# A two-layer graph network on one core: index work and layer 1's folds moved behind layer 0's table, the table's rows moved into x's memory, three x loads issued by ScalarE, and superchunks 3 to 5 gathered in place

## The chip, the cores and the metric

The kernel runs on one core of a Trainium2 chip. The metric is device time in microseconds (us) of one execution; three runs of the kernel before took 4008.17, 4010.82 and 4012.63 us. Changes are judged against the median, 4010.82.

TensorE (PE) multiplies, VectorE (DVE) and ScalarE (ACT) do element-wise work, GpSimd (POOL) here mainly issues gathers by index, and SyncE (SP) issues plain transfers. Each engine works through its own instructions in order and waits for others by semaphores.

## What is computed

There are 6250 nodes with 256 features, and 200000 edges sorted by destination, each with 32 attributes. The reference, cut to what matters:

```python
h = jnp.maximum(_layernorm(x, axis=-1), 0.0)

def _gat(x, src, dst, ea, Wg, a_s, a_d, Wge, a_e, b, n, h, f):
    hx = (x @ Wg).reshape(n, h, f)
    he = (ea @ Wge).reshape(-1, h, f)
    al = jax.nn.leaky_relu(jnp.einsum('nhf,hf->nh', hx, a_s)[src] + jnp.einsum('nhf,hf->nh', hx, a_d)[dst] + jnp.einsum('ehf,hf->eh', he, a_e), 0.2)
    m = jax.ops.segment_max(al, dst, num_segments=n)
    al = jnp.exp(al - m[dst])
    al = al / jax.ops.segment_sum(al, dst, num_segments=n)[dst]
    out = jax.ops.segment_sum(hx[src] * al[:, :, None], dst, num_segments=n)
    return out.reshape(n, h * f) + b

# per layer: te = relu(edge_attr @ We + be) * exp(x @ Wo + bo)[src], self loops added,
# layer 0 (4 heads): x = relu(_gat(...) + x); layer 1 (1 head): x = _gat(...) + x
x = x + (layer 1's x + h)
```

So each layer needs, for every edge, the row of its source node (`hx[src]` and a few numbers beside it), a softmax over the edges of one destination, and a weighted sum.

## The kernel before

**Prologue (`prologue`, L219).** The nodes are 49 tiles of 128 (`NT`), taken in groups of up to seven (`GT`), nine groups in all: tiles 0-1, 2-6, 7-13, 14-20, 21-27, 28-34, 35-41, 42-46 and 47-48. Per tile: layer norm statistics on VectorE (`stats`: bn_stats L292, bn_aggr L295, then an inverse square root by three Newton steps, on VectorE or for some groups on GpSimd, L307 to L325), normalisation and relu on ScalarE (`norm`, L337), two transposes on TensorE (`turn`, L343) and their copy on ScalarE (L345), a product with the weights (`mult`, L471), and the addition of the bias into a row block `trow` on VectorE (`keep`, L475). When a group is complete, `store` takes two exponentials on ScalarE (L360, L361) and writes the block into layer 0's table T0 in HBM (L362, on SP). The x blocks are loaded by SP (`load`, L241): six at the start and three more when a buffer comes free.

The edges are 1563 chunks of 128, in 66 superchunks of up to 24 chunks (C). Superchunk 0's source rows are not fetched from the table: GpSimd gathers their x from the input (`first_rows`, L275) into the buffer `G0`, and tiles 49 to 72 (groups 9 and 10) compute their rows in the same way, into `G0` itself.

`fold` (L187) and `fold_e` (L202) multiply attention vectors into the weights: four or two transposes, a ScalarE copy, a few small products, small copies on VectorE. `indices` (L477) and `index_group` (L630) load index tables and make the masks, offsets and flags that the edge loop needs, on VectorE; two of their results, `locrow` and `flags`, go to HBM and come back by `load_lb` and `load_fl`. These pieces are generators: the loop over tiles calls `next` on them at set values of its counter k, and so writes out by hand what stands between the tiles on each engine. In iteration k, tile k+3 is normalised, k+1 turned, k multiplied and k-1 kept.

**Edge loop (`edges`, L679).** A step is one superchunk of one layer. `gather` (L962) issues one indirect transfer per chunk on GpSimd, 128 rows of the table into the step's buffer G. There are three buffers (`gath0` to `gath2`), used in turn; `gath1` and `gath2` lie on memory that the prologue's pools had. Normally a step's first gather waits until the buffer's former step is done with all of it, that is with its sums; a step with `own` instead writes into that very tile, and each chunk's gather waits only for what used that chunk. Before, step 3 of layer 0 is such a step. VectorE makes one-hot matrices (`onehots`, L1163) and scaled rows (`scale`, L1334), and TensorE sums a step's edges into its nodes by one product a chunk (`sums`, L1353). Step k+1 is gathered while step k is computed. `ending` (L793) handles the last three superchunks a, b, c of a layer together and starts the next layer; layer 1's table T1 is written there by `rows3`.

Of the kernel before, what the change touches and what calls it, by code (L numbers as in the profile page):

```python
# [22 lines left out]
F32 = mybir.dt.float32  # L23
# [56 lines left out]
class Kernel:  # L80
# [138 lines left out]
    def prologue(self):  # L219
# [7 lines left out]
        with ExitStack() as c:  # L227
            xp = self.pool("x", 1, c)
            wp = self.pool("pw", 2, c)
# [6 lines left out]
            def load(g):  # L236
                if g < g0:
# [3 lines left out]
                    nc.sync.dma_start(x, a["x"][0:NT * P, :].rearrange("(p t) d -> p t d", p=P)[:, ts[0]:ts[0] + n, :])  # L241
# [26 lines left out]
            trows = [wp.tile([P, GT, L.TW], F32, name=f"trow{i}", bufs=1) for i in range(3)]  # L268
# [15 lines left out]
            def stats(g):  # L284

                n, x = len(groups[g]), xs[g]
                w = GT if g < g0 else C
                st = wp.tile([P, w, 6], F32, name=f"st{w}", bufs=2 if g < g0 else 1)
                mv = wp.tile([P, w, 2], F32, name=f"mv{w}", bufs=3 if g < g0 else 1)
                s = wp.tile([P, 3, w], F32, name=f"sc{w}", bufs=3 if g < g0 else 1)  # L290
                for i in range(n):
                    V.bn_stats(st[:, i, :], x[:, i, :])  # L292
                    yield
# [12 lines left out]
                e = nc.gpsimd if 3 <= g <= g0 else V  # L306
                for _ in range(3):  # L307
                    e.tensor_mul(t, y, y)
                    if e is V:
                        yield  # L310
                    e.tensor_mul(t, t, v)
                    if e is V:
                        yield
                    if e is V:
                        V.scalar_tensor_tensor(y, t, 1.5, y, op0=OP.add, op1=OP.mult)
                        yield
# [49 lines left out]
            ahead = {g: stats(g) for g in range(1, len(groups))}  # L366
# [4 lines left out]
            def step(g):  # L371

                for q in list(ahead):
                    if q > g if q < g0 else k < (16 if q == g0 else NT):
                        continue
# [7 lines left out]
            for k in range(-3, len(tiles) + 1):  # L383
                if k == 6:
# [7 lines left out]
                if k == 8:  # L392
# [8 lines left out]
                if k in (14, 26, 32):  # L401
                    drain(folds.pop())
                if k == 26:
# [1315 lines left out]
```

## Time and profile before

| | us |
|---|---|
| runs | 4008.17, 4010.82, 4012.63 |
| profiled execution | 4009.49 |
| its span | 4007.7 |
| GpSimd busy in the span | 3000.5 |
| TensorE busy | 2654.4 |
| VectorE busy | 2446.4 |
| ScalarE busy | 1120.2 |

A row of the groups gives line, engine, operation, output and inputs, count, then busy time and mean of one in ns, then the idle time just before them on that engine and what ended it. A row of the timeline gives start and duration in us, engine and line, and in brackets the idle time before with what ended it. A product in float32 runs as two passes and counts twice (x4 for two products). Times are counted from the span's start.

### The profile page before, as it was taken

To read this page: it belongs to the slowest core of one execution; us is meant where nothing else is said; L and a number is where in the kernel's file an instruction comes from. 1 tells how busy PE (TensorE), PEld (TensorE's weight loads), DVE (VectorE), ACT (ScalarE), POOL (GpSimd) and SP (SyncE) were. 2 spreads that over 40 slices of the span, in tenths; PEclk is the share of its full clock that TensorE was granted. 3 is DMA by queue.
4 is the path that set the end of the run, shared out by engine and by line. 5 is a ranking of instruction groups with operands and counts; after the bars stand their busy time and mean duration, and the time that the engine had idled before them with its cause. 6 is when DMAs were issued, how large, how long until landed. Compare 5 with 4: busy or idle time off the path is not lost. (4 is left out here: it accounts for less than half of the span.)

```text
span 4007.7 us, 37932 instructions
## 1 busy us (share of the span) xinstructions
PE 2654.4 (66%) x10018; PEld 1741.3 (43%) x10018; DVE 2446.4 (61%) x6074; ACT 1120.2 (28%) x2676; POOL 3000.5 (75%) x3264
## 2 busy tenths in 40 slices
PE   8777676676666666666786666666565665665665
PEld 6444444444444444444454343343343343343343
DVE  7798877877877877877874443443443443443445
ACT  6211111111111111111124343343343343343341
POOL 6777777777777777777777777777777777777775
PEclk9888888888888888888898777777777777777777
DMA  7555555555555555555555445445445545545553
GB/s 245 139 163 150 154 160 147 152 160 148 151 161 149 151 160 150 151 160 149 153 168 144 132 138 143 134 138 145 132 139 143 134 138 144 132 138 143 133 139 97
DMA packets 248103, 592.01 MB, mean 148 GB/s; under 512 B 65851, under 2 KB 105329, under 8 KB 247643
## 3 DMA queue, kind: packets, MB, share of 16 engines
q0 software_dynamic: 150144, 422.75, 40.8%
q1 hardware_dynamic: 97197, 166.49, 13.0%
q8 instruction: 86, 1.41, 0.1%
q14 instruction: 132, 1.08, 0.1%
q10 hardware_dynamic: 544, 0.28, 0.0%
HBM read 544.19 MB, written 45.46 MB: 147 GB/s over the span
## 5 line engine op out<-in xcount | busy, mean ns | idle before, releaser
L971 POOL DMA_INDIRECT G<-T,src x3078 | 2923.8, 950 | 949.6 <-issue 898.1
L1353 PE MATMUL u<-G,S 128*128 128x270 f32 (+1 forms) x6226 | 1567.4, 415 | 192.1 <-DVE G L1324 190.7
L1353 PEld LDWEIGHTS u<-G,S 128*128 128x128 f32 x6226 | 1275.5, 206 | 483.3 <-DVE G L1324 217.4
L1343 ACT ACTIVATE G<-G,kw 128x256 f32<-128x256 f32 x1512 | 609.0, 496 | 0.0
L1072 ACT ACTIVATE R<-y,webd 128x1024 f32<-128x1024 f32 (+2 forms) x264 | 235.5, 892 | 1274.9 <-PE y L1071 795.2
L1250 PE MATMUL lf<-ident,fb 128*36 128x128 f32 (+1 forms) x132 | 49.8, 377 | 766.2 <-DVE fb L1243 764.0
L1226 DVE TENSOR_TENSOR G<-rt,G 128x96 f32<-128x96 f32 (+1 forms) x132 | 30.3, 229 | 806.7 <-DMA G<-T,src 806.1
L1334 DVE TENSOR_TENSOR G<-G,kps 128x6144 f32<-128x6144 f32 (+3 forms) x79 | 441.0, 5593 | 0.0
L1163 DVE TENSOR_TENSOR S<-kps,loc 128x3072 f32<-128x3072 f32 x132 | 437.6, 3315 | 4.6
L1071 PE MATMUL y<-ea,webd 64*128 64x256 f32 (+1 forms) x1056 | 386.0, 825 | 50.2 <-ACT R L1072 50.2
L1080 PE MATMUL zad<-R,wea 128*64 128x384 f32 (+1 forms) x1056 | 301.7, 712 | 157.8 <-ACT R L1072 157.6
L1250 PEld LDWEIGHTS lf<-ident,fb 128*36 128x36 f32 (+1 forms) x132 | 15.7, 119 | 807.2 <-DVE fb L1243 804.1
L1080 PEld LDWEIGHTS zad<-R,wea 128*64 128x64 f32 x1056 | 86.5, 185 | 418.0 <-ACT R L1072 333.7
L1358 ACT ACTIVATE U<-u 128x270 f32<-128x270 f32 (+1 forms) x131 | 51.5, 393 | 631.6 <-PE u L1353 631.6
L1385 DVE SCALAR_TENSOR_TENSOR mg<-U,mw 128x1 f32<-128x1 f32 x66 | 14.6, 221 | 281.1 <-ACT mw L1383 281.1
L1071 PEld LDWEIGHTS y<-ea,webd 64*128 64x128 f32 x1056 | 123.0, 285 | 122.1 <-ACT R L1072 68.8
L1316 DVE SCALAR_TENSOR_TENSOR G<-U,kw,G 1x257 f32<-1x257 f32 x62 | 29.6, 477 | 184.3 <-ACT G L1343 184.3
L1212 DVE STREAM_TRANSPOSE rt<-zad 128x768 f32<-128x768 f32 (+1 forms) x130 | 126.0, 970 | 5.0 <-PE zad L1198 5.0
L471 PE MATMUL fin<-wg,h1T 128*128 128x260 f32 x264 | 122.6, 611 | 3.6 <-ACT h1T L1445 3.6
L1184 PE MATMUL zad<-a,Q 128*128 128x12 bf16 (+1 forms) x132 | 25.9, 197 | 148.5 <-DVE a L1179 148.1
L1095 DVE TENSOR_TENSOR lb<-lb,kps 128x1536 bf16<-128x1536 bf16 (+1 forms) x68 | 112.9, 1661 | 0.0
L1455 ACT ACTIVATE t1row<-t1row 128x1 f32<-128x1 f32 x66 | 13.4, 203 | 354.1 <-DVE t1row L475 354.0
(231 smaller groups left out, 2349.1 us busy)
## 6 DMA issues: line engine op xcount, KB each, us to landing
G<-T,src POOLq DMA_INDIRECT x3078, 2.8
ea<-in_ea_dram SPq DMA_DIRECT2D x64, 768.0 KB
lb<-locrow SPq DMA_DIRECT2D x64, 384.0 KB
nd<-t1row SPq DMA_DIRECT2D x66, 225.8 KB
tw<-nd SPq DMA_DIRECT2D x66, 225.8 KB
tw<-T SPq DMA_DIRECT2D x66, 117.2 KB
T<-t1row SPq DMA_DIRECT2D x66, 113.8 KB
tw<-in_x_dram SPq DMA_DIRECT2D x66, 112.0 KB
```

The source lines that it names most:

```text
L471: self.nc.tensor.matmul(ps[:, :L.MW], hT[:, k, :], self.wg[L.l][:, k, :], start=(k == 0), stop=(k == 1))
L971: nc.gpsimd.indirect_dma_start(out=G[:, c, 0:L.TW], out_offset=None, in_=st.get("from", self.T[L.l])[0:self.N, :], in_offset=bass.Indirect ...
L1071: nc.tensor.matmul(y[:, i, :n], self.webd[l][r, :], ea[r, w], start=True, stop=True)
L1072: nc.scalar.activation(R[:, :, w], y[:, :, :n], AF.Relu, bias=self.be[l])
L1080: nc.tensor.matmul(st["zad"][i * PH:(i + 1) * PH, o], self.wea[l][0], R[:, i, w], start=True, stop=False)
L1095: V.tensor_tensor(lb[:, :, :n], lb[:, :, :n], self.k_part.unsqueeze(2).to_broadcast([P, i, n]), op=OP.is_equal)
L1163: nc.vector.tensor_tensor(st["S"][:, c0:c1, :], self.k_iota.unsqueeze(1).to_broadcast(w), self.loc[:, o + c0:o + c1].unsqueeze(2).to_broad ...
L1212: V.transpose(rv[:, :32 * c].rearrange("p (b n) -> p b n", b=2), z.rearrange("p (b n) -> p b n", b=2)[:, :, :16 * c])
L1250: self.nc.tensor.transpose(self.lf[0:e.shape[1], 1:P + 1], e, self.ident)
L1334: nc.vector.tensor_tensor(v, v, pw[:, c0:c1, :].unsqueeze(3) .to_broadcast([P, c1 - c0, H, L.F]), op=OP.mult)
L1343: self.nc.scalar.activation(v, v, AF.Copy, scale=st["w"][:, c:c + 1])
L1353: nc.tensor.matmul(st["u"][:, :L.W], S[:, i, :], G[:, i, 0:L.W], start=(j == 0), stop=(j == c - 1))
```

## The change

- `trows`, the three row blocks, are allocated in x's pool instead of the working pool.
- `load` issues the blocks 6 to 8 on ScalarE's queue, right behind the normalisation that frees their buffer.
- `stats` takes several groups at once: groups 7, 8 and 9 (13 tiles) become one; the inverse root of group 3 runs on VectorE, of groups 4 to 9 on GpSimd, of group 10 (18 tiles of superchunk 0) on VectorE as before, and that group's statistics begin at k = 45.
- The index loads move from k = 6 to k = 28, the index steps on VectorE to after k = 50; the three folds beside the table (k = 12, 24, 30) move to k = 53, 56 and 61; three idle products of 512 columns are put at k = 1.
- The last row block of the table is kept and stored first thing in iteration 49.
- The gathers of x rows for superchunk 0 come earlier in GpSimd's order.
- Steps 3, 4 and 5 of layer 0 gather in place into the buffers of steps 0, 1 and 2.
- In `ending`, the second half of the next layer's `rphase1` (`drain(y)`: two products and a relu of 1024 columns) moves from ahead of superchunk b's rows to behind superchunk c's.

```diff
             xp = self.pool("x", 1, c)
+            trows = [xp.tile([P, GT, L.TW], F32, name=f"trow{i}") for i in range(3)]
...
-                    nc.sync.dma_start(x, a["x"][0:NT * P, :].rearrange("(p t) d -> p t d", p=P)[:, ts[0]:ts[0] + n, :])
+                    q = nc.scalar if g > 5 else nc.sync
+                    q.dma_start(x, a["x"][0:NT * P, :].rearrange("(p t) d -> p t d", p=P)[:, ts[0]:ts[0] + n, :])
...
-            def stats(g):
+            def stats(*gs):
...
-                e = nc.gpsimd if 3 <= g <= g0 else V
+                e = nc.gpsimd if 4 <= g <= g0 else V
...
-            ahead = {g: stats(g) for g in range(1, len(groups))}
+            q = max(g0 - 2, 2)
+            ahead = {g: stats(g) for g in range(1, q)}
+            ahead[q] = stats(*range(q, g0 + 1))
+            for g in range(g0 + 1, len(groups)):
+                ahead[g] = stats(g)
...
-                if k == 6:
+                if k == 28:
                     next(index)
...
-                if k > 16 and k % 2 or k > NT:
+                if k > NT + 1:
                     next(index, None)
-                if k == 5:
+                if k == 1:
+                    idle(3)
+                if k == 34:
                     more()
...
-                if k in (12, 24, 30):
-                    folds.append(fold(self.L[1], pt) if k == 24 else fold_e(self.L[k // 30], pt))
+                f = k - NT
+                if f in (4, 7, 12):
+                    folds.append(fold(self.L[1], pt) if f == 7 else fold_e(self.L[f // 12], pt))
                     next(folds[0])
...
+                if f == 0:
+                    keep(*tiles[k - 1])
+                    while kept < g0:
+                        store(kept)
+                        kept += 1
+                    self.load_ea(0)
...
-                    if i == 0:
-                        if g > 2:
-                            load(g + 3)
...
+                    if g > 1 and i == len(groups[g]) - 1:
+                        load(g + 4)
...
-                if 0 <= k < 10 or k >= 14 and k % 4 == 0:
+                if k < 9 or k >= 14 and k % 2:
                     next(rows0, None)
-                if k == max(NT - 6, 7):
+                if f == 12:
                     while not hasattr(self, "flags"):
                         next(index)
                     next(index)
+                    self.load_lb(0)
+                    self.load_fl(0)
...
-        if len(steps) > 3 and steps[3]["L"].l == 0:
-            steps[3]["own"] = self.G0
...
+            if 3 <= k + 1 < 6 and nx["L"].l == 0:
+                nx["own"] = steps[k - 2]["G"]
             self.gather(nx)
...
         if after:
             self.rows3(a)
-        drain(y)
         self.rows1(b)
...
         self.rows3(c)
+        drain(y)
```

TensorE around tile 13 before, the place of layer 0's `fold_e` (`wge` is its weight, `h` and `hT` a normalised tile and its transpose, `ps` a product's bank):

```order
L471 MATMUL ps<-wg_99,hT 128x266 x2
L182 MATMUL pT<-ident,wge 128x128 x2
L209 MATMUL ps<-att_100,hT 128x4 x2
L343 MATMUL pT<-ident,h 128x128 x2
L471 MATMUL ps<-wg_99,hT 128x266 x2
```

And now at tiles 52 to 57, behind the table's 49 tiles:

```order
L479 MATMUL ps<-wg_102,hT 128x266 x2
L182 MATMUL pT<-ident,wge 128x128 x2
L209 MATMUL ps<-att_103,hT 128x4 x2
L340 MATMUL pT<-ident,h 128x128 x2
L479 MATMUL ps<-wg_102,hT 128x266 x2
L340 MATMUL pT<-ident,h 128x128 x2
L479 MATMUL ps<-wg_102,hT 128x266 x2
L340 MATMUL pT<-ident,h 128x128 x2
L479 MATMUL ps<-wg_102,hT 128x266 x2
L182 MATMUL pT<-ident,wg_882 128x128 x4
L194 MATMUL ps<-att_883,hT 128x2 x4
```

Between tiles 2 and 48 nothing but the tiles' own transposes and products stands on TensorE now.

VectorE at the end of the table, before (`trow` receives a table tile, `G` a tile of superchunk 0; slink, qd and low are index results):

```order
L561 TENSOR_TENSOR slink<-sc_389 1x66
L475 TENSOR_TENSOR trow_198<-ps,bias_105 128x266
L475 TENSOR_TENSOR trow_199<-ps,bias_105 128x266
L567 TENSOR_TENSOR qd_1223<-scf 1x264
L569 TENSOR_TENSOR low<-sc_389 1x66
L475 TENSOR_TENSOR trow_199<-ps,bias_105 128x266
L292 BN_STATS st_1235<-G 128x6 x4
```

And now:

```order
L483 TENSOR_TENSOR trow_82<-ps,bias_108 128x266
L294 BN_STATS st_1056<-G 128x6 x4
L483 TENSOR_TENSOR trow_82<-ps,bias_108 128x266
L294 BN_STATS st_1056<-G 128x6 x4
L483 TENSOR_TENSOR G<-ps,bias_108 128x266
L294 BN_STATS st_1056<-G 128x6 x2
L297 BN_AGGR mv_1057<-st_1056 128x2 x8
L504 CAST scf<-sc_782 128x726
```

The statistics of superchunk 0's later tiles stand ahead of the last table tile's addition, and the first index step (L504) behind it.

GpSimd's first gathers of layer 0, one row per step from step 1 on, with buffer numbers; before:

```order
L971 DMA G_1655<-T0_60,src_165 128x268 x24
L971 DMA G_1776<-T0_60,src_165 128x268 x24
L971 DMA G_201<-T0_60,src_165 128x268 x24
L971 DMA G_2085<-T0_60,src_165 128x268 x24
L971 DMA G_2254<-T0_60,src_165 128x268 x24
L971 DMA G_2429<-T0_60,src_165 128x268 x24
```

And now:

```order
L979 DMA G_1612<-T0_60,src_168 128x268 x24
L979 DMA G_1733<-T0_60,src_168 128x268 x24
L979 DMA G_201<-T0_60,src_168 128x268 x24
L979 DMA G_1612<-T0_60,src_168 128x268 x24
L979 DMA G_1733<-T0_60,src_168 128x268 x24
L979 DMA G_2384<-T0_60,src_168 128x268 x24
```

Steps 4 and 5 now write into the same tiles as steps 1 and 2 (G_1612, G_1733) instead of new ones; step 3 into superchunk 0's (G_201) as before; from step 6 on each step has a new tile again.

More of the change, by code (lines that the diff above doesn't have):

```diff
@@ L267, in prologue @@
                 nc.sync.dma_start(self.T[0][NT * P:N + P, :], zero[:N + P - NT * P, :L.TW])
-            trows = [wp.tile([P, GT, L.TW], F32, name=f"trow{i}", bufs=1) for i in range(3)]
             ln = wp.tile([P, NT + CX, 2], F32, name="ln", bufs=1)
@@ L282, in prologue @@
                 next(rows0, None)
-            def stats(g):
[L286 to L293, printed above, removed]
+            def stats(*gs):
+                n, g = sum(len(groups[g]) for g in gs), gs[0]
+                w = GT if n <= GT else C
+                st = wp.tile([P, w, 6], F32, name=f"st{w}", bufs=2)
+                mv = wp.tile([P, w, 2], F32, name=f"mv{w}", bufs=3 if w < C else 2)
+                s = wp.tile([P, 3, w], F32, name=f"sc{w}", bufs=3 if w < C else 2)
+                for q in sorted(gs, key=lambda q: q == g0 - 1):
+                    for i in range(len(groups[q])):
+                        V.bn_stats(st[:, groups[q][i] - groups[g][0], :], xs[q][:, i, :])
+                        yield
                 for i in range(n):
@@ L373, in step @@
                 for q in list(ahead):
[L374 removed]
+                    if q > g if q < g0 else k < NT - 4:
                         continue
@@ L409, in prologue @@
                     if i == 0:
-                        if g > 2:
-                            load(g + 3)
                         drain(ahead.pop(g, ()))
                     norm(g, i, t)
+                    if g > 1 and i == len(groups[g]) - 1:
+                        load(g + 4)
                 if k < NT - 1:
                     step(g + 2)
-                if 0 <= k - 1 < len(tiles):
+                if 0 <= k - 1 < len(tiles) and f:
                     keep(*tiles[k - 1])
```

15 lines of the change are left out of this document (3 added, 12 removed).

## The prediction

> **What bounds the kernel now.** I read the busy line first, then GpSimd's groups and waits, then its timeline at both ends.
>
> ```profile
> PE 2654.4 (66%) x10018; PEld 1741.3 (43%) x10018; DVE 2446.4 (61%) x6074; ACT 1120.2 (28%) x2676; POOL 3000.5 (75%) x3264
> L971 POOL DMA_INDIRECT G<-T,src x3078 | 2923.8, 950 | 949.6 <-issue 898.1 <-PE u L1353 8.2 <-DMA fl<-flags 6.4
> POOL G L971 <- DMA T<-t1row: 2.5, 1, 2.5
> 82.63 0.94 POOL L971 DMA_INDIRECT G<-T,src  x1 [6.39 <-DMA fl<-flags]
> 113.17 0.95 POOL L971 DMA_INDIRECT G<-T,src  x1 [0.85 <-ACT G L356]
> 143.25 0.95 POOL L971 DMA_INDIRECT G<-T,src  x1 [0.30 <-PE u L1353]
> 172.57 0.95 POOL L971 DMA_INDIRECT G<-T,src  x1 [0.30 <-issue]
> 176.92 0.94 POOL L971 DMA_INDIRECT G<-T,src  x1 [3.40 <-PE fin L1443]
> 3979.12 0.94 POOL L971 DMA_INDIRECT G<-T,src  x1 [0.30 <-issue]
> ```
>
> POOL is 75% busy, yet it is the bound: nearly all of its idle time before the gathers is 0.30 us of issue after each (898.1 of 949.6). A gather costs 0.95 + 0.30 = 1.25 us and the stream has no holes worth naming but three: 0.85 us at 113.17, 3.40 at 176.92, and the 2.5 behind the last table store of layer 0. So time = start of the first table gather (82.63) + a stream that ends at 3979.12 + 0.94 = 3980.1 + a tail to 4007.7. Only three things can move the end: the first start, the holes, and what an earlier start runs into. The four rows 82.63, 113.17, 143.25 and 176.92 are the first gathers of steps 1, 2, 3, 4 of layer 0; the last gather of step 3 is at 172.57, so step 4 wanted to start at 173.8.
>
> The execution took 4009.49 us, 1.8 more than its span and 1.3 below the median of the runs, 4010.82. I count differences on the span and subtract them from the median.
>
> **The change part by part.**
>
> *The table earlier.* Before the table is complete, TensorE paces the prologue.
>
> ```profile
> 9.55 1.17 PE L471 MATMUL ps<-wg,hT 128*128 128x266 f32 x4
> 13.52 0.44 PE L343 MATMUL pT<-ident,h 128*128 128x128 f32 x2 [2.79 <-ACT h L337]
> 13.79 1.95 PE L471 MATMUL ps<-wg,hT 128*128 128x266 f32 x4
> 28.23 0.38 PE L182 MATMUL pT<-ident,wge 128*128 128x128 f32 x2
> 30.50 0.61 PE L209 MATMUL ps<-att,hT 128*128 128x4 f32 x4 [1.89 <-ACT hT L184]
> 34.91 0.38 PE L343 MATMUL pT<-ident,h 128*128 128x128 f32 x2
> 46.10 0.60 PE L182 MATMUL pT<-ident,wg 128*128 128x128 f32 x4
> 54.69 0.38 PE L182 MATMUL pT<-ident,wge 128*128 128x128 f32 x2
> 76.48 1.07 PE L471 MATMUL ps<-wg,hT 128*128 128x266 f32 x4
> ```
>
> From 34.91 to 46.10 ten tiles take 11.19 us: 1.12 us a tile, with no gap. Tile 2 is turned at 13.52. Tile 48, the last of the table, is multiplied at 76.48, and turned one tile (1.12 + 0.22) earlier, at 75.14. The 46 tiles between cost 61.6 us where 46 x 1.12 = 51.5 would do: 10.1 us lost, at four places that the rows show: the 2.79 us gap and the slow clock after it (1.95 us for four passes that later take 1.07), and the three folds at 28.23 (with its 1.89 wait), 46.10 and 54.69. All three folds move behind the table. The gap is filled by three idle products: six passes over 512 columns at 1.07/4/266 us a column are 3.1 us, from 10.72 to 13.8; were they slow it would be up to 2.4 us more, which the row at 9.55 (1.17, almost full speed) speaks against. So tile 48 is turned at 13.8 + 51.5 = 65.3 at best.
>
> Not quite that: group 3's rsqrt steps come back from POOL to VectorE, and group 4's still run on POOL.
>
> ```profile
> 35.71 0.21 POOL L308 TENSOR_TENSOR sc<-sc 128x7 f32<-128x7 f32 x1 [4.93 <-DVE sc L302]
> 40.01 0.25 POOL L325 TENSOR_SCALAR ln<-sc 128x7 f32<-128x7 f32 x1
> 20.32 0.16 DVE L322 SCALAR_TENSOR_TENSOR ln<-mv,sc 128x7 f32<-128x7 f32 x1
> 45.42 0.43 DVE L292 BATCH_NORM_STATS2 st<-x 128x6 f32<-128x256 f32 x1 [1.70 <-DMA x<-in_x_dram]
> 0.74 0.45 ACTq L128 DMA_DIRECT2D wg<-in_wg_dram  x1
> ```
>
> Walking VectorE's new order with these durations from 20.32 (about 1.3 us earlier now, its two waits on slow products gone): groups 3 and 4 with the stores between them reach POOL at about 31.4, POOL's chain takes 4.5, so tile 21 is normalised at 36.3 where TensorE wants it at about 35.3; tile 28 is some 0.2 late, later ones are not. Bounds: nothing, and 3 us. I take 1.5: tile 48 turned at 66.8, multiplied by 69.2. The x loads cost ScalarE three issues of 0.45 us in 0.84 of work per 1.12; nothing, and the 1.70 us wait at 45.42 has no successor.
>
> ```profile
> 77.58 0.43 DVE L475 TENSOR_TENSOR trow<-ps,bias 128x266 f32<-128x266 f32 x1 [0.16 <-PE ps L471]
> 77.93 1.39 DVE L292 BATCH_NORM_STATS2 st<-G 128x6 f32<-128x256 f32 x4
> 79.00 0.19 ACT L361 ACTIVATE trow<-trow 128x2 f32<-128x2 f32 x1
> 73.36 6.19 SPq L362 DMA_DIRECT2D T<-trow  x3
> ```
>
> Today the last row block is added at 77.58, exponentiated at 79.0, its store issued by 79.55, and the first gather comes at 82.63: 3.4 us from issue to gather. In the new order the add stands behind four bn_stats (1.39 us, 0.33 apart), so at 69.9; exponentials follow at once; issue at 70.6; first gather at 74.0, 8.6 us earlier.
>
> *Rows in x's memory.* Step 2's first gather waited for ScalarE's last prologue instruction (113.17): its buffer lay on the working pool. With 22.5 KB more in x's pool both gather buffers lie on it. No wait is left: 0.55 us gained, and without this part step 2 would stall until the prologue's end.
>
> *What the prologue's end now is.* All index work is done beside the 24 tiles of superchunk 0.
>
> ```profile
> 84.93 1.28 DVE L295 BATCH_NORM_AGGREGATE mv<-st 128x2 f32<-128x6 f32 x18
> 86.83 0.17 DVE L308 TENSOR_TENSOR sc<-sc 128x18 f32<-128x18 f32 x1
> 88.82 0.17 DVE L322 SCALAR_TENSOR_TENSOR ln<-mv,sc 128x18 f32<-128x18 f32 x1
> 89.68 0.69 PE L343 MATMUL pT<-ident,h 128*128 128x128 f32 x2 [6.54 <-ACT h L337]
> 93.34 0.38 PE L343 MATMUL pT<-ident,h 128*128 128x128 f32 x2
> 113.00 1.75 DVE L1095 TENSOR_TENSOR lb<-lb,kps 128x1536 bf16<-128x1536 bf16 x1
> 139.07 13.48 PE L1353 MATMUL u<-G,S 128*128 128x270 f32 x48 [0.95 <-DVE G L1334]
> 163.75 12.89 PE L1353 MATMUL u<-G,S 128*128 128x270 f32 x48 [3.39 <-DVE G L1324]
> 213.73 13.70 PE L1353 MATMUL u<-G,S 128*128 128x270 f32 x48 [4.75 <-DVE G L1324]
> ```
>
> VectorE is solid from about 66: 15 bn_stats (5.0), six adds (2.0), the aggregates (1.3), first index steps (1.2), the rsqrt (86.83 to 88.99, with its three steps ahead 2.7) end near 78. So TensorE stalls again, some 6 us, and resumes at 79.9 with tile 54 (before: tile 55 at 89.68). From there the 19 tiles (21.3), the slow restart (two tiles in 3.66 instead of 2.24: 1.4), the folds of layer 1 (3.2 by the places at 46.10 and 54.69) and the last product (1.2) end at 107.0; the last add and seven index steps end at 108.7, where VectorE starts step 0: 4.3 us before today's 113.00. Step 0's sums then start at 139.07 - 4.3 = 134.8. Bounds of that 4.3: zero, if locrow's store and lb's load, now made after the lrow steps at about 88, were not landed by 108; and 6, if the rsqrt ends sooner.
>
> *What the earlier gathers run into.* Step 3 gathers into superchunk 0's buffer, chunk by chunk behind its products. Today it came at 143.25, 3.3 us after it could (139.07 + 0.56 for a chunk + 0.3). Now it would come at 74.0 + 60.07 = 134.1 and may start at 134.8 + 0.9 = 135.7: **a new wait of 1.6 us**. Products go at 0.56 us a chunk, gathers at 1.25, so only the first waits. Step 4 no longer waits for the whole of step 1's sums: the 3.1 us beyond issue go (its first product is done near 160). Step 4 starts at 135.7 + 30.57 (143.25 to 173.8) = 166.3 instead of 176.92: **10.6 us**. Step 5 is far from its sums. Step 6 waits again for a whole buffer: step 3's sums end at 213.73 + 13.7 - 4.3 = 223.1, its gather comes at about 226.7. Compute needs about 25 us a step against 30 of gathers, so the lag is made up and the rest of the stream shifts as it is.
>
> *The layer's end.* One relu of 1.11 us leaves ScalarE's queue in front of superchunk b's and c's steps.
>
> ```profile
> 2041.45 1.11 ACT L1072 ACTIVATE R<-y,webd 128x1024 f32<-128x1024 f32 x1 [0.41 <-PE y L1071]
> 2042.97 0.16 DVE L1397 TENSOR_TENSOR mg<-U,mw 128x4 f32<-128x4 f32 x1 [0.85 <-ACT mw L1395]
> ```
>
> VectorE's 0.85 wait shrinks to the usual 0.28 and the next add's 0.34 goes: 0.9 us of the 2.5 (bounds 0 and 2.2). The product and relu land under the wait for the table rows.
>
> Sum: 10.6 + 0.9 = 11.5; 4010.82 - 11.5 = 3999.3.
>
> A rule against the change: the Trainium skill, page "SBUF — State Buffer", section "SBUF: two separate sides", says VectorE and GpSimd share a port pair under an exclusive lock, also for VectorE instructions with two SBUF inputs, and the loser blocks fully. The index steps now run beside gathers.
>
> ```profile
> 171.10 1.16 POOL L971 DMA_INDIRECT G<-T,src  x1 [0.30 <-issue]
> 171.03 0.42 DVE L1513 TENSOR_TENSOR t1row<-tw,hw 128x256 f32<-128x256 f32 x1
> ```
>
> Beside an add of two SBUF tensors a gather took 1.16 instead of 0.95. Some twelve such index steps newly meet gathers: 2.5 us at 0.21 each, of which 1.6 vanish in the wait at step 3.
>
> **The rivals.**
>
> 1. *The table bounds, not step 0*: step 0's sums start before 133.2. For it: bounds of the 4.3. Then step 4 starts at 74.0 + 60.07 + 30.57 = 164.6, a gain of 12.3 + 0.9: 3997.6; with no lag at tile 21, 3996.
> 2. *Step 0 is not earlier*: the prologue's end stays at 113 because index work, folds and lb's round trip fill what was gained. Step 3 waits until 140.0, step 4 starts at 170.5: gain 6.4 + 0.9, 4003.5. For it: VectorE and TensorE both have more to do after the table than before.
> 3. *Gathers slowed by VectorE* as in the rule: 1 us net, 4000.3.
> 4. *Slower*: after the stall near 73 to 79 TensorE does not get its clock back, since its tiles are now interrupted by folds that wait for ScalarE. At the slow clock of 13.79 a tile takes 1.12 x 1.95/1.07 = 2.04 us; 19 of them cost 17.5 us more, less the 0.7 counted, step 0's sums start at 151.6, 12.5 after today's, and the kernel takes 4010.82 - 6.4 - 0.9 + 12.5 = 4016. It decides from 0.6 us more per tile (11.5/19). Against it: today the clock is back after two tiles.
> 5. *The gain is not there*: step 2's gather still waits for the prologue's end (107): 104.1 becomes 107.5, step 4 at 168.1, gain 8.8 + 0.9: 4001.1. Against it: x's pool is now 58 KB, two gather buffers 52.
>
> **How the numbers follow.** Forecast 50%, rival 1 12%, 2 17%, 3 6%, 4 8%, 5 3%, and 4% for small losses that I don't see. 0.2% is 8.0 us, about what a measurement of this kernel can tell from no change: faster below 4002.8. The forecast, 1, 3 and 5 are faster (71%), and a small part of 2; the rest of 2 and 4% are within; 4 is slower, and 1% more. Faster 0.73, same 0.18, slower 0.09. Range: rival 1's best, 3995, to a step 0 that is 2 us later than today, 4010.82 - 6.4 - 0.9 + 2 = 4005.5.
>
> **What would show it.** First table gather at about 74 and step 2's without a wait at 104; a wait of 1 to 3 us before step 3's first gather on TensorE's sums; no 3.4 us wait before step 4's; TensorE stalled some 6 us around 73 to 79 and step 0's sums at about 135; the wait behind T<-t1row near 1.6. I am wrong if the first gather comes after 78, if step 0's sums start after 139, or if a new wait appears before step 6's gather.

## The result: 4002.88 us, a gain of about half the forecast

The changed kernel takes 4002.88 us (median of 17 runs, 3998.99 to 4006.20), the kernel before, on the same chip, 4008.84 (17 runs, 4006.77 to 4012.63). The ratio is 0.9984 with a 95% interval of 0.9978 to 0.9991: faster by 6.0 us, or 0.16%. The interval excludes a ratio of 1, so there is a gain, but its size stays within the 0.2% that the prediction called no change. Forecast were 3999.3 and 11.5 us. The sign is right, and nearly half of the size is missing. The time lies in the range, but with little room: counted from this median of 4008.84 instead of 4010.82, the range would have ended at 4003.5.

The profiled execution took 4002.88 us with a span of 4000.6 (before: 4009.49 and 4007.7). GpSimd's timeline after, with the rows that answer to those of before: the first gathers of steps 1, 2, 3 and 4 of layer 0, the first of layer 1 from the main table, and the last.

```profile
74.47 1.07 POOL L979 DMA_INDIRECT G<-T,src  x1 [14.99 <-ACT hT L342]
104.96 0.94 POOL L979 DMA_INDIRECT G<-T,src  x1 [0.30 <-issue]
137.05 0.94 POOL L979 DMA_INDIRECT G<-T,src  x1 [2.38 <-issue]
167.36 0.94 POOL L979 DMA_INDIRECT G<-T,src  x1 [0.30 <-PE u L1361]
2045.67 0.95 POOL L979 DMA_INDIRECT G<-T,src  x1 [2.35 <-DMA T<-t1row]
3970.45 0.95 POOL L979 DMA_INDIRECT G<-T,src  x1 [0.30 <-issue]
```

| Lead over before, us | forecast | measured |
|---|---|---|
| first gather (82.63) | 8.6 | 8.16 |
| step 3's first (143.25) | 7.55 | 6.20 |
| step 4's first (176.92) | 10.6 | 9.56 |
| what the layer's end adds | 0.9 | 0.27 |
| last gather (3979.12) | 11.5 | 8.67 |
| span (4007.7) | 11.5 | 7.1 |

(The layer's end: the lead was 7.51 at layer 0's step 61 and 7.78 at the first step behind the boundary.) So the new start does nearly what was worked out for it, and the difference is made up of three leaks: 1.0 us up to step 4; 1.8 between step 4 and the last gather (layer 0 loses 2.05 from there on, the boundary between the layers gives 0.6 less than forecast, and layer 1 gives 0.9 back); 1.6 behind the last gather. The last 1.1 us between 7.1 and the medians' 6.0 is less than the runs scatter.

The three engines of the prologue after, TensorE first. The rows are the transposes and the product of tile 48 (a tile's product stands behind the next tile's transposes), the fold that now stands behind the table, its stalled product, the first tile behind it, and step 0's sums.

```profile
67.04 0.38 PE L340 MATMUL pT<-ident,h 128*128 128x128 f32 x2
...
68.38 1.06 PE L479 MATMUL ps<-wg,hT 128*128 128x266 f32 x4
...
74.32 0.38 PE L182 MATMUL pT<-ident,wge 128*128 128x128 f32 x2
79.17 1.02 PE L209 MATMUL ps<-att,hT 128*128 128x4 f32 x4 [4.48 <-ACT hT L184]
80.05 0.67 PE L340 MATMUL pT<-ident,h 128*128 128x128 f32 x2
135.56 11.21 PE L1361 MATMUL u<-G,S 128*128 128x270 f32 x48 [0.95 <-DVE G L1342]
```

And VectorE: four statistics of superchunk 0 ahead of the last table tile's addition, that addition, the end of group 10's rsqrt, the last addition of the prologue and the first operation of step 0.

```profile
68.78 1.39 DVE L294 BATCH_NORM_STATS2 st<-G 128x6 f32<-128x256 f32 x4
70.10 0.41 DVE L483 TENSOR_TENSOR trow<-ps,bias 128x266 f32<-128x266 f32 x1
78.05 0.17 DVE L319 SCALAR_TENSOR_TENSOR ln<-mv,sc 128x18 f32<-128x18 f32 x1
107.59 0.43 DVE L483 TENSOR_TENSOR G<-ps,bias 128x266 f32<-128x266 f32 x1 [0.30 <-PE ps L479]
109.43 1.78 DVE L1103 TENSOR_TENSOR lb<-lb,kps 128x1536 bf16<-128x1536 bf16 x1
```

The reader sees the forecast's shape: the addition of tile 48 behind the statistics (69.9 forecast, 70.10 measured), the rsqrt's end at 78, the stall of TensorE (6 us forecast, 4.5 measured, resumed at 79.2 instead of 79.9), step 0 on VectorE at 109.43 (108.7), its sums at 135.56 (134.8), and the new wait of step 3's gather on them.

### The profile page after: what moved, and what is told of

Same layout as the page of the kernel before. It is cut to its first block, busy times and chain, and to the rows that moved or that the text cites. A ratio compares the mean times of both kernels' runs of the same rounds, so it can differ in the third digit from the quotient of the medians.

```text
span 4000.6 us, 37931 instructions
## 1 busy us (share of the span) xinstructions
PE 2660.5 (67%) x10024; PEld 1745.8 (44%) x10024; DVE 2448.1 (61%) x6079; ACT 1120.0 (28%) x2676; POOL 2990.7 (75%) x3219
```

## Experiments on a chip like the first

Each kernel ran 11 times beside 33 runs of the kernel before on one chip, where that took 4014.14 us (4009.0 to 4019.48). Ratios are to it; the changed kernel's 0.9984 was measured on the first chip. Of the profiles only the first 300 us are compared to a tenth of a microsecond (the section on the hardware says why).

**Steps 4 and 5 with new tiles.**

```diff
-            if 3 <= k + 1 < 6 and nx["L"].l == 0:
+            if k + 1 == 3 and nx["L"].l == 0:
                 nx["own"] = steps[k - 2]["G"]
```

> The changed kernel, but steps 4 and 5 of layer 0 take new gather tiles again; only step 3 is in place. Theory 1 (the whole-buffer wait): step 1's sums end at 171.1 in the changed kernel's trace, and step 4's first gather, which came at 167.36, waits for them and comes at 171.5; a wait of about 4.4 us before it, no other new one, and the time goes up by 4.1, to 4007.0: two thirds of the whole gain hang on these two lines. Theory 2 (the wait is made up later, since 30 us of gathers per step meet 25 us of compute): the hole appears and later steps give it back; within 1 us of 4002.9.

4010.55 us, ratio 0.9992 (0.9983 to 1.0001). Step 4's first gather, GpSimd's timeline:

```profile
172.12 0.95 POOL L979 DMA_INDIRECT G<-T,src  x1 [4.58 <-PE fin L1451]
```

Theory 1 holds in the trace: the wait is back at 4.58 us, longer than the 3.40 of before, because the gathers come earlier and step 1's sums by less. 4.76 us are lost at step 4 (0.49 of them already at step 3, whose plan is the same: so much does one plan scatter), and 4.94 are still lost at steps 5 and 6: nothing is given back. The ratio is 3 us worse than the changed kernel's, with intervals that overlap, and its own interval no longer excludes 1. So about half of the lead at step 4 (4.3 to 4.8 of 9.56 us) hangs on the two in-place tiles.

**The row tiles back on the working pool.**

```diff
-            trows = [xp.tile([P, GT, L.TW], F32, name=f"trow{i}") for i in range(3)]
             wp = self.pool("pw", 2, c)
...
+            trows = [wp.tile([P, GT, L.TW], F32, name=f"trow{i}", bufs=1) for i in range(3)]
             ln = wp.tile([P, NT + CX, 2], F32, name="ln", bufs=1)
```

> The changed kernel with the three row tiles back on the prologue's working pool. Theory 1: step 2's gather buffer then overlaps the working pool, so its first gather waits for the prologue's last instruction on that pool, between 107 (TensorE's last product) and 109.4 (VectorE's last index step), where it came at 104.5 without a wait; step 3 then starts at 107.3 + 30.7 = 138.0 to 140 instead of 137.05, since 2.4 us of its wait vanish: 1.0 to 3 us slower, 4003.9 to 4006. Theory 2: the tiles' place decides nothing, no wait before step 2, within 0.5 us.

4010.46 us, ratio 0.9990 (0.9981 to 0.9999). Step 2's first gather:

```profile
111.31 0.94 POOL L979 DMA_INDIRECT G<-T,src  x1 [6.25 <-issue]
```

The wait is there, so theory 1; but it ends 1.9 us behind the upper bound that I gave it. The trace calls it issue; in the program the instruction waits, among others, for VectorE's last index step, which ended at 110.37 here, 0.9 us before. Step 3 then starts at 141.31, 4.26 later than in the changed kernel, since now the stream and not step 0's sums sets it. The place of the rows is worth about as much as the in-place tiles.

**Layer 0's fold in front of the table again.**

```diff
-                if f in (4, 7, 12):
+                if k == 12 or f in (7, 12):
...
-                if f in (6, 9, 14):
+                if k == 14 or f in (9, 14):
```

> The changed kernel with layer 0's fold of the edge weights back in front (at tile 12, as before the change). Theory 1 (step 0's sums bind the stream at step 3, not the table): the fold takes TensorE 1.0 to 3 us away before the table, so the first gather comes at 75.5 to 77.5 instead of 74.47, but the wait before step 3 shrinks by the same, step 3's first gather stays at 137.0 or comes up to 1 us earlier, because TensorE has the fold no longer behind the table; time 4002 to 4003.5. Theory 2 (the table binds): 1 to 3 us slower, 4003.9 to 4006.

4005.74 us, ratio 0.9980 (0.9971 to 0.9989). The first gathers of steps 1 and 3 (GpSimd's timeline):

```profile
74.94 1.08 POOL L979 DMA_INDIRECT G<-T,src  x1 [14.75 <-ACT h L334]
135.82 0.95 POOL L979 DMA_INDIRECT G<-T,src  x1 [0.30 <-issue]
```

TensorE's timeline of the same kernel: the fold's product in front, the tile on which TensorE now waits behind the table, and step 0's sums.

```profile
27.42 0.61 PE L209 MATMUL ps<-att,hT 128*128 128x4 f32 x4 [0.47 <-ACT hT L184]
79.47 0.44 PE L340 MATMUL pT<-ident,h 128*128 128x128 f32 x2 [3.16 <-ACT h L334]
133.69 11.21 PE L1361 MATMUL u<-G,S 128*128 128x270 f32 x48 [1.21 <-DVE G L1342]
```

The table gets 0.47 us later, not 1 to 3, although TensorE spends 1.32 on the fold (from 26.56 to the next tile at 27.88). On VectorE's timeline of the changed kernel no gap stands between 25.85 and 36.58, so VectorE paces that stretch too, which would hide most of a pause of TensorE there. Step 0's sums come 1.87 earlier, the wait before step 3 is gone, and step 3 starts 1.23 **earlier** than in the changed kernel. Theory 1 holds, and by more than it claimed: up to step 4 (166.23 against 167.36) moving this fold behind the table was a loss. There its product waits 4.48 us in TensorE's queue for a copy by ScalarE that stands behind the stalled normalisation, and all of it lies in front of step 0. In the ratios the loss can't be told from nothing, since the intervals overlap.

**Index work two tiles later, then two steps a tile.**

```diff
-                if k > NT + 1:
+                if k > NT + 3:
                     next(index, None)
+                if k > NT + 14:
+                    next(index, None)
```

> The changed kernel with the index work begun two tiles later, behind superchunk 0's last rsqrt, and two steps of it per tile from tile 64 on. Theory 1 (VectorE's queue sets step 0's start, and step 0's sums set step 3's gathers): 1.2 us of index steps leave the way of the rsqrt, so TensorE's wait of 4.48 us shrinks to about 3.3, and no index step is left behind the last addition, 1.4 us more; step 0's sums start at 133 instead of 135.56, the wait of 2.38 us before step 3 shrinks to under 0.6, and step 3 comes 2 us earlier: 4000.9. Theory 2 (another resource ends step 0's start): the sums stay at 135 or later, same time within 0.5 us or slower.

4005.44 us, ratio 0.9977 (0.9968 to 0.9986). TensorE's stalled product and step 0's sums, then step 3's first gather (two timelines of this kernel):

```profile
78.17 1.02 PE L209 MATMUL ps<-att,hT 128*128 128x4 f32 x4 [3.38 <-ACT hT L184]
133.61 6.65 PE L1363 MATMUL u<-G,S 128*128 128x270 f32 x28 [0.95 <-DVE G L1344]
```

```profile
135.19 0.95 POOL L981 DMA_INDIRECT G<-T,src  x1 [0.30 <-issue]
```

Theory 1 holds: rsqrt's end and TensorE's resumption 1.0 us earlier, sums 1.95 earlier, no wait before step 3, which starts 1.86 earlier and 60.71 behind the first gather (74.48), the bare stream. VectorE's queue, not TensorE's work, set step 0's start; from here on the table's end is the bound. By its ratio it is 3 us better than the changed kernel, and its profile shows where 1.86 of them come from; it has the lowest ratio of the versions tried, though the intervals overlap.

## Experiments on two other chips

The next runs came to two other chips, with a mean granted clock of 0.72 instead of 0.79. On the first of them the kernel before takes 4802 us (4804 and 4805 beside the second and third run of a kernel), and **there the change costs 1.4%**. The clock is used here as a name for these chips; the traces don't show it to be the cause. It reads 0.50 between 120 and 140 us in the kernel before on the first chip too, where TensorE waits 3.5 us at most.

| Kernel | us, median (range) | ratio to before, 95% |
|---|---|---|
| before | 4802.26 (4799.12 to 4813.13) | |
| changed_again | 4864.46 (4863.87 to 4881.68) | 1.0141 (1.0124 to 1.0158) |
| in_place_alone | 4828.58 (4819.18 to 4832.65) | 1.0053 (1.0039 to 1.0066) |
| in_place_alone_2 | 4827.76 (4826.85 to 4830.29) | 1.0050 (1.0036 to 1.0065) |
| early_stats | 4856.31 (4847.08 to 4863.34) | 1.0107 (1.0091 to 1.0122) |
| early_stats_2 | 4857.98 (4849.23 to 4866.57) | 1.0112 (1.0095 to 1.0129) |
| early_stats_3 | 4860.94 (4858.14 to 4863.66) | 1.0120 (1.0103 to 1.0137) |
| adds_doubled | 4872.01 (4866.02 to 4878.30) | 1.0143 (1.0128 to 1.0159) |

The kernels' own questions had been put for a chip like the first, and most were left without an answer.

**The changed kernel again** (no edit).

> The changed kernel itself once more, beside the others on one chip. Theory 1 (the gathers' pace differs from one execution to the next, and the plan of the first 200 us doesn't): first gather within 0.2 us of 74.47, step 3's within 0.5 of 137.05 and step 4's within 0.5 of 167.36, while the last gather may stand up to 5 us later than 3970.45. Theory 2: the early lead itself scatters by a microsecond or more.

Neither theory could be tested: the first gather came at 90.12, step 2's at 120.99, step 3's at 205.84. TensorE's windows by stretch (busy us and count, granted clock, DMA share, GB/s) and its timeline show what happened between:

```profile
40.00:80.00 40.00, 39.84 (x211) 1.00 0.80 251
80.00:120.00 40.00, 24.70 (x102) 0.72 0.49 150
120.00:160.00 40.00, 8.25 (x21) 0.50 0.37 98
```

```profile
123.63 2.14 PE L479 MATMUL ps<-wg,hT 128*128 128x266 f32 x4 [9.14 <-issue]
138.98 2.14 PE L479 MATMUL ps<-wg,hT 128*128 128x266 f32 x4 [12.78 <-issue]
155.83 2.14 PE L479 MATMUL ps<-wg,hT 128*128 128x266 f32 x4 [14.28 <-ACT hT L342]
```

Three tiles of superchunk 0 take 12 to 17 us each, at a granted clock of 0.50; from 166.72 on a product takes 1.06 us again. TensorE's transposes ahead of the product at 138.98, and ScalarE's copy of them, show on which way the time goes:

```profile
125.56 0.64 PE L340 MATMUL pT<-ident,h 128*128 128x128 f32 x2
138.54 0.39 ACT L342 ACTIVATE hT<-pT 128x256 f32<-128x256 f32 x1 [14.48 <-issue]
```

The transposes are recorded as done at 126.20 and the copy starts 12.3 us later, while the product that needs the copy starts 0.05 us behind the copy's end (138.93). So it is what TensorE hands on that comes late, not what it is handed. GpSimd's rows around it:

```profile
149.79 0.95 POOL L979 DMA_INDIRECT G<-T,src  x1 [0.30 <-issue]
205.84 0.95 POOL L979 DMA_INDIRECT G<-T,src  x1 [55.09 <-issue]
```

The 48 gathers of steps 1 and 2 end at 150.74, and TensorE is free 5 us later. In the kernel with only the in-place tiles the gathers stop at 118.26, after step 1, because step 2's buffer still lies on the working pool; TensorE's last wait of over 2 us there ends at 122.78. In the kernel before, on the other chip of clock 0.72, they stop at 120.28 and the wait ends at 123.17. In all eight traces from these two chips TensorE is held up while gathers run, and its last long wait ends 1 to 8 us behind the last of them. The same is seen earlier: in changed_again the first gathers of x end at 27.87, a product waits until 31.40, and by then 14.5 of the 15.65 us are lost by which the first table gather is late (90.12 against 74.47).

On such a chip the rows in x's memory, which save a wait elsewhere, let 24 more gathers run beside the prologue: step 3 starts at 205.84 instead of 175.63. The distance stays: it is 41 us at step 8 and 38 at the last gather, and the medians lie 36 apart. That the rows' place alone is the cause was not tried there; rows_on_work_pool ran on the other kind of chip.

**Steps 4 and 5 in place, alone** (the kernel before with the two lines on `own`), twice.

> The kernel before with only steps 4 and 5 of layer 0 put in place; the prologue and the layer's end as before. Theory 1 (the whole-buffer wait): step 4's first gather comes at 173.8 instead of 176.92, the 3.4 us wait there is 0.3, everything behind it 3.1 us earlier: 3.1 us faster than before, ratio 0.9992. Theory 2 (step 5 or 6 waits instead, and the lead is given back there): within 1 us of before.

> The kernel of in_place_alone once more, on another chip: the kernel before with only steps 4 and 5 of layer 0 put in place. Theory 1 (the whole-buffer wait): step 4's first gather comes at 173.8 instead of 176.92, the 3.4 us wait there is 0.3, everything behind it 3.1 us earlier: 3.1 us faster than before, ratio 0.9992. Theory 2 (step 5 or 6 waits instead, and the lead is given back there): within 1 us of before.

The second run came to the same chip. 0.5% slower both times. GpSimd's timeline of the first: the first gathers of steps 4, 5 and 6.

```profile
209.84 1.05 POOL L971 DMA_INDIRECT G<-T,src  x1 [4.11 <-PE u L1353]
254.84 0.95 POOL L971 DMA_INDIRECT G<-T,src  x1 [14.85 <-PE u L1353]
311.04 0.95 POOL L971 DMA_INDIRECT G<-T,src  x1 [24.38 <-PE fin L1443]
```

Nearer to theory 2, though a loss and not the same time: step 4 waits for its first chunk alone, but steps 5 and 6 stand for 15 and 24 us. On a chip like the first this part was measured only by taking it out.

**The kernel before, for a trace** (no edit).

> The kernel before itself, for a trace of it on the chip of 4802 us, where the changed kernel takes 4864 and the one with only steps 4 and 5 in place 4828. Theory A (on that chip a gather that runs in place, chunk by chunk beside the sums whose tile it fills, costs more than the wait it removes): step 3 starts within 4 us of 177, step 4 near 212, and steps 5 and 6 follow 35 us apart instead of 45 and 56, so that step 6 starts at 282 to 288 where in_place_alone started it at 311 to 316, and the distance is kept to the end. Theory B (the 25 us are lost elsewhere, a little in each step): step 6 starts at 305 or later and the distance grows along both layers. On a chip of 4009 to 4014 us instead: the trace of before within 0.5 us up to step 4's first gather at 176.92.

One execution, 4915.31 us, and on yet another chip of clock 0.72 (the run beside it took 4906.79), so its time says nothing beside the table; up to step 6 the trace can be read.

```profile
176.46 0.95 POOL L971 DMA_INDIRECT G<-T,src  x1 [4.59 <-PE u L1353]
226.40 0.95 POOL L971 DMA_INDIRECT G<-T,src  x1 [20.17 <-PE fin L1443]
260.92 0.95 POOL L971 DMA_INDIRECT G<-T,src  x1 [4.71 <-PE fin L1443]
296.05 0.94 POOL L971 DMA_INDIRECT G<-T,src  x1 [5.13 <-PE u L1353]
```

Half of theory A: steps 5 and 6 follow 34.5 and 35.1 us apart and step 6 starts 15 to 20 us before in_place_alone's (311.04 and, in its second run, 316.32); but step 4 came 14 us later than said, and later steps ran at another pace than on the chip of 4802 us, so that the distance behind step 6 can't be compared. Where the 25 us go on the chip of 4802 us stays open.

**Superchunk 0's statistics eight tiles earlier**, three times, all on the chip of 4802 us.

```diff
-                    if q > g if q < g0 else k < NT - 4:
+                    if q > g if q < g0 else k < NT - 12 or k == NT - 1:
...
                 if k > NT + 1:
                     next(index, None)
+                if k > NT + 14:
+                    next(index, None)
```

> The changed kernel with the statistics of superchunk 0's later tiles taken eight tiles earlier, into VectorE's gaps of 0.68 us around 56 to 64 (none at the last table tile), and two index steps per tile from tile 64 on. Theory 1 (VectorE's queue, not TensorE's work, sets when step 0 starts; with it out of the way the table's end is the bound): the rsqrt ends near 73 instead of 78, TensorE's wait of 4.48 us in front of the fold's product falls under 1.5, the last table addition stands behind no bn_stats, so the first gather comes at 73.8 to 74.1 instead of 74.47; step 0's sums start at 130.5 to 132.5 instead of 135.56; no wait before step 3, which starts 60.7 after the first gather, at 134.6; step 4 at 164.9 instead of 167.36. Gain over the changed kernel 2.4 us. Theory 2 (TensorE and ScalarE set it): sums later than 133.5, first gather as it was, gain under 1.9.

> The kernel of early_stats once more, on another chip (the one before took 4802 us for the kernel before, and there signals between engines came up to 16 us late beside gathers, so that no time of its first 200 us can be compared). Theory 1 (VectorE's queue sets when step 0 starts; with it out of the way the table's end is the bound): TensorE's wait of 4.48 us in front of the fold's product falls under 1.5, the first gather comes at 73.8 to 74.1 instead of 74.47, step 0's sums start at 130.5 to 132.5 instead of 135.56, no wait before step 3, which starts at 134.6, step 4 at 164.9 instead of 167.36: 2.4 us faster than the changed kernel, ratio to before about 0.9978. Theory 2 (TensorE and ScalarE set it): sums later than 133.5, first gather as it was, gain under 1.9.

> The kernel of early_stats a third time. The two runs so far were on a chip where the kernel before takes 4802 us and signals between engines come up to 16 us late beside gathers. If the chip is one where the kernel before takes 4009 to 4014 us: theory 1 (VectorE's queue sets when step 0 starts; with it out of the way the table's end is the bound): first gather at 73.8 to 74.1 instead of 74.47, step 0's sums at 130.5 to 132.5 instead of 135.56, no wait before step 3, which starts at 134.6, step 4 at 164.9 instead of 167.36; ratio to before about 0.9978. Theory 2 (TensorE and ScalarE set it): sums later than 133.5, first gather as it was, gain under 1.9. If it is a chip of 4802 us again: 1.011 as before.

The first step of theory 1 shows even there: TensorE's wait before the fold's product, 4.33 us in the changed kernel on that chip, is 0.53. The rest, and whether it beats the changed kernel on a chip like the first, stays open: on that chip its medians lie 4 to 8 us below the changed kernel's and 54 to 56 above those of the kernel before beside it (4802.26, 4803.91 and 4804.72). These expectations speak of late signals between engines. The rows of changed_again narrow that down to what TensorE hands on; the ends of TensorE's rows are modelled, so whether its signals were late or TensorE itself stood still, the traces don't tell.

**The addition made twice.**

```diff
         e.tensor_add(nrow, st["xw"], st["hw"])
+        e.tensor_add(nrow, st["xw"], st["hw"])
         yield
```

> The changed kernel with the addition of t1row<-tw,hw made twice for each step (the second writes the same values again). Theory 1 (a gather that meets an addition of two SBUF tensors takes 0.21 us longer): in the changed kernel's trace 28 of the 66 such additions overlap a gather of over 1.05 us, so 64 more give 20 to 27 more slow gathers than 53 (47 in layer 0), layer 0's gathers end 4 to 5.7 us later, ratio to the changed kernel 1.001. Theory 2 (slow gathers only happen to stand beside it): 45 to 60 slow ones as before, time within 1 us.

Gathers of over 1.05 us, counted in GpSimd's timeline: 90 (74 of them in layer 0), against 59 (34) for the changed kernel on the same chip. The groups of gathers by line, first of the changed kernel there, then of this one:

```profile
L979 POOL DMA_INDIRECT G<-T,src x3078 | 2931.7, 952 | 1768.5 <-issue 940.5 <-PE zad L1192 339.5 <-PE fin L1451 206.7
```

```profile
L979 POOL DMA_INDIRECT G<-T,src x3078 | 2937.2, 954 | 1773.4 <-issue 943.6 <-PE zad L1192 343.6 <-PE u L1361 198.1
```

5.5 us more in the gathers themselves, with only VectorE's work altered. Theory 2 is out: there are 31 more. Theory 1 comes near (20 to 27 were said), but mostly by luck. The gathers that start 0.05 to 0.20 us behind the start of such an addition are 18 instead of 11, and all of them are slow. Another 19 instead of 2 start as close behind a different addition of two SBUF tensors, G<-G,crow, and all of these are slow too: the second addition moved what stands behind it against the gathers. The time, 7.6 us more than the changed kernel's, goes the same way, but the two intervals overlap almost whole.

## Why the forecast was right, and where it was too large

*The table earlier*: 74.0 forecast, 74.47 measured. Tile 48 was to be turned at 66.8 and was at 67.04, its addition at 69.9 and was at 70.10; the way from there to the first gather was 0.3 longer than said. Inside, the pieces moved: the idle products ended at 12.94 instead of 13.8, and TensorE lost 2.3 us against its bare pace (13.21 + 46 x 1.12 = 64.7) where 1.5 were taken and 3 was the bound. One price was wrong in its form: the fold at 28.23 was counted as lost time of TensorE, and fold_in_front shows 0.47 us for it at the table. In the new order VectorE is as full as TensorE in that stretch.

*Rows in x's memory*: as forecast, no wait at step 2; rows_on_work_pool shows the price without it, 4.3 us at step 3.

*Step 0's sums and the new wait*: forecast 134.8 and 1.6, measured 135.56 and 2.1 (2.38 less the 0.30 of issue). The place, the cause and the order of size are right. The sums were 0.8 later, 0.7 of it already at VectorE's start of step 0 (109.43 for 108.7), and the first gather came 1.5 behind their start, not 0.9. That is the 1.35 us missing at step 3; from there to step 4 it took 30.31 us instead of 30.57, which leaves 1.0. index_later and fold_in_front confirm what the forecast rested on, that step 0 and not the table was the bound: each takes 1.9 us off step 0 and removes the wait. Rival 1 is out; rival 2 (step 0 not earlier) too: it is 3.5 us earlier.

*Step 4's wait gone*: as forecast; with new tiles there is a wait of 4.58 us.

*The layer's end*: 0.27 instead of 0.9, and the wait behind T<-t1row is 2.35 instead of 2.54, where 1.6 was forecast. What was to shrink did: VectorE's wait of 0.85 is 0.28. The step that failed is TensorE's speed, which the sum took as unchanged. TensorE's product for superchunk b and VectorE's addition behind it, before and then after:

```profile
2042.89 1.14 PE L471 MATMUL fin<-wg,h1T 128*128 128x260 f32 x4 [1.12 <-ACT h1T L1445]
2044.07 0.43 DVE L475 TENSOR_TENSOR t1row<-fin,bias 128x260 f32<-128x260 f32 x1 [0.34 <-PE fin L471]
```

```profile
2033.92 2.10 PE L479 MATMUL fin<-wg,h1T 128*128 128x260 f32 x4 [0.53 <-ACT h1T L1453]
2036.06 0.43 DVE L483 TENSOR_TENSOR t1row<-fin,bias 128x260 f32<-128x260 f32 x1 [1.16 <-PE fin L479]
```

The granted clock between 2033 and 2037 was 0.50, where it had been 1.00. From the first to the last of the three additions it took 9.37 us instead of 8.24. new_tiles_4_5 has the same layer's end, kept its clock there (1.14 for this product), and took 7.38: 0.86 less than before, which is the forecast, and its wait behind T<-t1row is 1.01. In the other nine traces with the new order the product took 2.10, with the old order in one of four. So the forecast's price holds at full clock. That moving a product away makes the slow clock likelier fits these counts, but was not tried by itself; and the 0.27 is no sign of the term, since the stretch that it speaks of got longer.

*Slow gathers* (rival 3): right in kind, and put in the wrong place. I looked for them beside the twelve index steps; they come through the whole of layer 0. Both engines in the changed kernel's timeline:

```profile
466.42 0.42 DVE L1521 TENSOR_TENSOR t1row<-tw,hw 128x256 f32<-128x256 f32 x1
466.50 1.16 POOL L979 DMA_INDIRECT G<-T,src  x1 [0.30 <-issue]
```

28 of the 66 such additions overlap a slow gather, one of over 1.05 us, against 17 before. The starts tell which instruction did it. Of the gathers that start 0.05 to 0.20 us behind the start of such an addition, 14 of 14 are slow, before 12 of 12, and in all fourteen traces 127 of 128. The other 14 of the 28 had begun ahead of the addition, and 13 of these start as close behind an earlier instruction, fb<-U,mw. So did the gather that the addition at 554.48 overlaps:

```profile
553.35 0.42 DVE L1434 TENSOR_TENSOR fb<-U,mw 128x256 f32<-128x256 f32 x1
553.42 1.18 POOL L979 DMA_INDIRECT G<-T,src  x1 [0.30 <-DMA G<-T,src]
```

A gather that began 0.45 us ahead of an addition (494.21, beside 494.66) took its usual 0.94. So it is a matter of phase: a gather that starts in the first 0.2 us of such an instruction takes 0.21 longer. Gathers over 1.05 us are 45 in layer 0 against 29, at 0.2 each 3 us, and 6 against 12 in layer 1, which gives 1 back. That covers the lead that melts between step 4 and the layer's end (9.56 to 7.51). Whether the change itself moved the gathers into a worse phase is not shown: in the four kernels on the chip of 4014 us, which share layer 0's code, the count was 31 to 38, so that 45 may be the chance of one execution. The Trainium skill, page "SBUF — State Buffer", section "SBUF: two separate sides", says that whichever of a VectorE instruction with two SBUF inputs and a GpSimd instruction that reads SBUF starts first has the shared port pair for its whole instruction, and the other fully blocks. Here the gather loses half of the addition's 0.42 us, and only if it starts in that first stretch.

*The tail*, from the last gather to the end: 28.6 before, 30.1 after, and the forecast had no such term. The first of the two last scatters comes 0.55 later behind the last gather, and the second stands 0.73 longer behind the first (3990.30, idle for 2.87 with its data ready at 3988.46); nothing in the trace releases it. The four kernels on the chip of 4014 us have tails of 28.6 to 30.0 with the same code, so it looks like scatter and not like an effect of the change.

*Rival 4*, TensorE without its clock behind the stall, did not come on the first chip: two slow tiles from 80.05, as before. On the chip of 4802 us the change is a loss, and TensorE loses its time at the place that this rival named; but the loss is waits of 9 to 14 us beside gathers, not the slow tiles (2.04 us each) that it counted, and so it is far larger than its 12.5 us. That it named the place is luck. It was weighed with 8% from a trace in which the clock returns after two tiles; that trace could not show that another chip behaves otherwise.

## What to carry to other kernels

When a stream of transfers is the bound, an earlier start is worth only what the buffers behind it can take: here the 8 us at the start became 9.6 at step 4, and would have been under 5 without either the tiles freed chunk by chunk or the rows' new place. Before moving an engine's work out of the way of a bound, look at which other engine paces that stretch: the fold cost TensorE time where VectorE had none to spare, so that it cost little in front of the table (0.47 us) and more behind it. And a gain of a few microseconds from overlap should be tried on more than one chip: the same change won 0.16% on one and lost 1.4% on another.

## What the hardware showed that was not expected

The pace of the gathers differs between executions by 2 to 3 ns each. The groups of GpSimd in layer 1 between 2200 and 3900 us, first of the changed kernel, then of index_later, whose code there is the same:

```profile
L979 POOL DMA_INDIRECT G<-T,src x1359 | 1286.8, 947 | 413.9 <-issue 405.1 <-DVE ade L1223 4.9 <-DVE rt L1220 3.7
```

```profile
L981 POOL DMA_INDIRECT G<-T,src x1356 | 1287.2, 949 | 413.3 <-issue 404.2 <-DVE ade L1225 7.0 <-DVE rt L1222 1.8
```

(1286.8 + 413.9) / 1359 is 1.2514 us a gather, (1287.2 + 413.3) / 1356 is 1.2541: over 3078 gathers 8 us, as much as the whole change. new_tiles_4_5 and fold_in_front ran at 1.2538, before and rows_on_work_pool at 1.2518 and 1.2517, the last on the same chip as the first two. It is why medians of many runs are needed here, and why only the first steps of two traces can be set side by side.

On the chip of 4802 us TensorE got through three tiles in 44 us while gathers ran, and what came late was what it handed on to ScalarE and VectorE; in the eight traces from chips with a mean granted clock of 0.72 it was free again 1 to 8 us behind the last gather. What holds it there was not tried.
